# Adding the interpolated biases to the logits on TensorE and ScalarE in the first image's layer 0

## The chip, the cores and the metric

The kernel is one program on one core of a Trainium2 chip. The metric is the device time in microseconds (us) of one execution; lower is better. Each engine of the core (TensorE, written PE in the profile; VectorE, DVE; ScalarE, ACT; GpSimd, POOL; SyncE, SP) works through a queue of its own in the order in which the queue was laid out, and engines wait for one another through semaphores.

## The reference, cut to what matters

The network has four layers over four images of 32 x 32 positions and 384 channels. The change touches only layer 0, an attention whose keys are sampled at learned positions. Cut to the lines that matter:

```python
q = jnp.einsum('bhwc,cd->bhwd', x, w_q) + b_q
...
k = (xs @ w_k + b_k).reshape(Bq, n, HEADS, HC)
v = (xs @ w_v + b_v).reshape(Bq, n, HEADS, HC)
attn = jnp.einsum('bmhc,bnhc->bhmn', qh, k) * scale
disp = (ref.reshape(1, n, 1, 2) - pos.reshape(Bq * G, 1, n, 2)) * 0.5
bias = _bilinear_sample(rpe_img, disp)
attn = jax.nn.softmax(attn + bias, axis=-1)
out = jnp.einsum('bhmn,bnhc->bmhc', attn, v)
```

There are 6 heads of 64 channels and n = 1024 positions. For each image and head, `attn` is 1024 x 1024, and so is `bias`: each entry is a bilinear interpolation in a table, with weights that depend on the key alone.

## The kernel before, in words

**Two lanes.** `Front` computes layer 0 of an image, `Trunk` layers 1 to 3. Both are generators of instructions. `Net.layer0` writes out the whole front of image 0 before anything else; from then on the trunk of image b is written out interleaved with the fronts of the later images. So layer 0 of the first image stands alone, and that of the other three shares the engines with the trunk of the image before.

**Order on the engines.** The framework, Tile, lays out each engine's queue when the kernel is built: earlier code goes first where it can, and later code is moved up into what the framework takes for a gap. The trace shows that the order isn't the one in the code. `keep_in_program_order` pins single instructions; none in `head0` is pinned. A tag of a tile pool is a fixed number of slots: `bank` has 4 PSUM slots of 128 x 512, `lg` 13 SBUF slots, `z` 3, `win` 4, `tb` 2.

**The pass.** `Front.layer0` calls `head0(h, q)` for 6 heads and 2 halves of the queries: 12 passes an image. Everything is transposed: keys lie on the 128 partitions, queries on the free axis. A pass has 8 key tiles j (128 keys each) and 512 queries.

- *Bias of one key tile* (L733 to L752): POOL gathers a window of the table for each key (`win`, L734); ACT multiplies by one weight into `z` (L746), DVE adds the other row (L747); ACT multiplies by the column weight into `lg` (L751), DVE adds the other column (L752). Now `lg` holds the interpolated bias, 128 x 512.
- *Logits* (L754 to L761): PE multiplies the keys with the queries into a `bank` (L755); DVE adds the bank to `lg`, in place (L756); DVE keeps a running maximum over the key tiles in `rmax` (L759, L761).
- *Maximum over keys* (L765 to L780): PE transposes `rmax` in four pieces into a bank (L768), DVE reduces it (L772), POOL spreads the result on diagonals (L774), PE multiplies those with ones to have the maximum of each query on all partitions (L776), ACT copies it to `tb` (L780).
- *Softmax and values* (L784 to L798): for each of the 8 tiles DVE subtracts `tb` (L787), ACT takes the exponential (L788), PE multiplies with the values and with ones into one bank, `po`, in its two halves of 64 partitions (L790). Then ACT copies the output over the queries in `qpad` (L794) and the sums out (L797), and a DMA on SP's queue stores the sums (L798).
- After every second head `over_sums` (L801 to L822) loads the sums, has DVE invert them (L808), stores them, loads them spread over partitions and has DVE multiply the outputs (L821).

A float32 matmul stands in the trace as two records of MATMUL and two of LDWEIGHTS. A slot of `lg` is free again when L790 has read its tile, so 5 tiles of the next pass can have their bias ready while the 8 of this pass are in use. After the 12 passes `l0c` projects the output (`dense_t`, L376), adds it to the input (L432) and stores it; the trunk of image 0 begins from that.

Of the kernel before, what the change touches and what calls it, by code (L numbers as in the profile page):

```python
# [21 lines left out]
ALU = mybir.AluOpType  # L22
# [4 lines left out]
P = 128  # L27
# [37 lines left out]
def bc(ap, axis, n):  # L65

    u = ap.unsqueeze(axis)
    shape = list(u.shape)
    shape[axis] = n
    return u.broadcast_to(shape)  # L70


class Net:
# [183 lines left out]
    def layer0(self, b):  # L257

        if b == 0:
            for _ in self.front.layer0(b):  # L260
                pass
            self.done = self.ahead = 0.0
            self.fronts = (w for i in range(1, NB) for w in self.front.layer0(i))
# [135 lines left out]
class Front(Lane):  # L399


    def layer0(self, b):
        nc, v = self.nc, self.nc.vector
        with self.scope("l0"):
            self.qpad = self.wt([P, KC, PW, PW], "qpad")
            nc.gpsimd.memset(self.qpad, 0.0)

            self.kz = [self.wt([P, N], f"kz{r}") for r in range(2)]
            for r in range(2):
                nc.gpsimd.memset(self.kz[r][GC * (1 - r) : GC * (2 - r), :], 0.0)  # L410
            self.va = self.wt([P, NJ, C], "va")
            self.f = self.wt([P, 2, 2, NJ * G], "bias_f")
            self.widx = self.wt([P, 2, NJ * G], "widx", 1, I32)
            with self.scope("l0a"):
                yield from self.inputs0(b)
            with self.scope("l0b"):
                self.load_keys(0)
                for h in range(G):
                    if h + 1 < G:
                        self.load_keys(h + 1)  # L420
                    for q in range(2):
                        yield from self.head0(h, q)
                    if h % 2:
                        yield from self.over_sums(h // 2)
            with self.scope("l0c"):
                w = self.weights("w_out")
                for ko in range(KC):
                    rows = slice(ko * P, (ko + 1) * P)
                    x = self.wt([P, N], "res", 2)
                    nc.sync.dma_start(x, self.x0[b % 2][rows, :])  # L430
                    ps = self.dense_t(w, self.qpad, ko)
                    v.scalar_tensor_tensor(x, ps, self.col(C_BOUT, ko), x, ALU.add, ALU.add)  # L432
                    nc.sync.dma_start(self.x1[b % 2][rows, :], x)
                    yield 6
# [281 lines left out]
        rows = slice((h % 2) * GC, (h % 2 + 1) * GC)  # L716
        self.nc.sync.dma_start(self.kz[h % 2][rows, :], self.k0[h * GC : (h + 1) * GC, :])

    def head0(self, h, q):

        nc, v = self.nc, self.nc.vector
        f, kz, va = self.f, self.kz[h % 2], self.va
        k, r0 = h // 2, (h % 2) * GC
        rows = slice(r0, r0 + GC)
        other = slice(GC - r0, 2 * GC - r0)
        HH, HN = HW // 2, N // 2
        both = self.qpad[:, k, 1 + HH * q : 1 + HH * (q + 1), 1 : 1 + HW]
        queries = both[rows]
        logits = []
        rmax = self.wt([P, HN], "rmax", 2)  # L730
        for j in range(NJ):
            c = j * G + h
            win = self.wt([P, (HH + 1) * WROW], "win", 4)  # L733
            nc.gpsimd.indirect_dma_start(  # L734
                out=win,
                out_offset=None,
                in_=self.strips[:, :],
                in_offset=bass.IndirectOffsetOnAxis(
                    ap=self.widx[:, q, c : c + 1], axis=0
                ),  # L740
            )
            wv = win.rearrange("p (r c) -> p r c", c=WROW)
            sc = lambda i, t: f[:, i, t, c : c + 1]

            z = self.wt([P, HH, HW + 1], "z", 3)
            nc.scalar.activation(z, wv[:, 0:HH, 0 : HW + 1], AF.Copy, scale=sc(1, 1))  # L746
            v.scalar_tensor_tensor(  # L747
                z, wv[:, 1 : HH + 1, 0 : HW + 1], sc(0, 1), z, ALU.mult, ALU.add
            )
            lg = self.wt([P, HH, HW], "lg", 13)  # L750
            nc.scalar.activation(lg, z[:, :, 0:HW], AF.Copy, scale=sc(1, 0))  # L751
            v.scalar_tensor_tensor(lg, z[:, :, 1 : HW + 1], sc(0, 0), lg, ALU.mult, ALU.add)  # L752
            lf = lg.rearrange("p y x -> p (y x)")
            ps = self.bank()  # L754
            nc.tensor.matmul(ps, kz[:, j * P : (j + 1) * P], both, start=True, stop=True)  # L755
            v.tensor_tensor(lf, ps, lf, ALU.add)  # L756
            logits.append(lf)
            if j == 1:
                v.tensor_tensor(rmax, logits[0], lf, ALU.max)  # L759
            elif j > 1:  # L760
                v.tensor_tensor(rmax, rmax, lf, ALU.max)  # L761
            yield 3


        NI = HN // P  # L765
        ps = self.bank()
        for i in range(NI):
            nc.tensor.transpose(  # L768
                ps[:, i * P : (i + 1) * P], rmax[:, i * P : (i + 1) * P], self.ident
            )  # L770
        top = self.wt([P, NI], "top", 2)
        v.tensor_reduce(top, ps.rearrange("p (i n) -> p i n", i=NI), AX.X, ALU.max)  # L772
        diag = self.wt([P, NI, P], "diag", 1)
        nc.gpsimd.tensor_tensor(diag, bc(self.ident, 1, NI), bc(top, 2, P), ALU.mult)  # L774
        ps = self.bank()
        nc.tensor.matmul(  # L776
            ps, self.ones, diag.rearrange("p i n -> p (i n)"), start=True, stop=True
        )
        tb = self.wt([P, HN], "tb", 2)
        nc.scalar.copy(tb, ps)  # L780
        yield 3


        po = self.bank()  # L784
        for j in range(NJ):
            lf = logits[j]
            v.tensor_tensor(lf, lf, tb, ALU.subtract)  # L787
            nc.scalar.activation(lf, lf, AF.Exp)  # L788
            for out, w in ((rows, va[:, j, h * GC : (h + 1) * GC]), (other, self.ones[:, 0:GC])):
                nc.tensor.matmul(po[out, :], w, lf, start=j == 0, stop=j == NJ - 1)  # L790
            if j % 2:
                yield 2

        nc.scalar.copy(queries, po[rows, :].rearrange("p (y x) -> p y x", y=HH))  # L794
        o0 = other.start
        den = logits[0][o0 : o0 + 1, :]
        nc.scalar.copy(den, po[o0 : o0 + 1, :])  # L797
        nc.sync.dma_start(self.den[h][:, q * HN : (q + 1) * HN], den)  # L798
        yield 3
# [753 lines left out]
```

## Time and profile before

| what | value |
|---|---|
| median of three runs | 5029.74 us (5029.07 to 5034.31) |
| the profiled execution: device time / span | 5029.6 us / 5027.8 us |
| PE, DVE, ACT, POOL busy in the span | 86%, 63%, 48%, 19% |
| the passes of the first image, 225 to 605 us | PE 234.5, DVE 312.6, ACT 197.3, POOL 127.0 us busy of 380 |
| L756 in the whole kernel | 384 of 684 ns |
| L755 in the whole kernel | 768 records of 623 ns |
| L780 in the first image | 12 of 586 ns |

The start of the 12 copies into `tb` (L780) marks the passes of the first image: 255.9, 286.8, 315.5, 343.1, 388.2, 417.6, 446.0, 475.2, 520.5, 549.3, 578.4 and 605.0 us. They are read in the timeline of ACT. Eleven periods follow the first pass: nine from 26.6 to 30.8 us, with a mean of 28.7 us, and two of 45.1 and 45.3 us, which follow the `over_sums` of heads 0, 1 and 2, 3.

How to read it: a line of the page's groups names the line of code, the engine, the operation, output and input, and the count; then the busy time and the mean of one in ns; then how long the engine stood idle just before, and whom it waited for. In a timeline, a line gives the start, the duration, the engine and the instruction, with "x8" for eight merged; in brackets stands the idle time before it. PEclk is the share of TensorE's full clock that was granted.

### The profile page before, as it was taken

Reading aid. Unit: us, or ns where it says so; the run is one execution under the profiler, and the core shown is the slowest. Engines: PE = TensorE matmul, PEld = TensorE weight load, DVE = VectorE, ACT = ScalarE, POOL = GpSimd, SP = SyncE. Lnnn points to the kernel's source line nnn. Section 1 sums busy time; section 2 is a strip of 40 time slices with the busy share of each in tenths; the row PEclk is TensorE's granted clock in tenths of the full one; section 3 lists DMA queues with packets and bytes.
Section 4 is the critical chain, followed back from the end, with each engine's and each line's share of the span. In section 5 each row is a group of like instructions: output and inputs, shape, how many; then the busy total and the mean of one; then the engine's idle time right before and its main releaser. Section 6 shows DMA issues by size and latency. Waiting matters only on the chain. (4 is left out here: it accounts for less than half of the span.)

```text
span 5027.8 us, 47291 instructions
## 1 busy us (share of the span) xinstructions
PE 4315.1 (86%) x15788; PEld 1843.8 (37%) x15788; DVE 3178.1 (63%) x5743; ACT 2404.6 (48%) x4346; POOL 944.7 (19%) x946
## 2 busy tenths in 40 slices
PE   4466587899999988899999989789999998899998
PEld 2222242333333353333333444233333335234444
DVE  3477727577778725567777752657776872555544
ACT  2155424466666213466665412446666621566630
POOL 1523202211212002321122110321121200000000
PEclk7677787899999988799999989689999998799998
DMA  6322252311212143222121124231121214101001
GB/s 116 108 77 84 66 163 66 105 53 50 70 50 72 38 136 108 79 87 60 50 70 56 50 80 144 68 102 50 50 71 50 72 36 134 58 19 29 23 29 38
DMA packets 226707, 360.57 MB, mean 72 GB/s; under 512 B 116323, under 2 KB 163520, under 8 KB 226464
## 3 DMA queue, kind: packets, MB, share of 16 engines
q1 hardware_dynamic: 165448, 191.06, 12.6%
q0 software_dynamic: 39936, 145.53, 10.0%
q10 hardware_dynamic: 21080, 20.96, 1.8%
q8 instruction: 125, 2.05, 0.2%
q14 instruction: 118, 0.97, 0.1%
HBM read 279.55 MB, written 78.21 MB: 71 GB/s over the span
## 5 line engine op out<-in xcount | busy, mean ns | idle before, releaser
L1206 DVE SCALAR_TENSOR_TENSOR e<-bank,gam,e 128x512 f32<-128x512 f32 x768 | 562.8, 748 | 552.2 <-ACT gn L1205 247.4
L1197 PE MATMUL bank<-sim,sg 128*128 128x512 f32 (+3 forms) x2304 | 853.7, 507 | 5.1 <-DVE e L1206 5.1
L1044 ACT ACTIVATE big<-big,nmax 128x512 f32<-128x512 f32 x768 | 508.7, 662 | 420.7 <-DVE nmax L1039 383.8
L734 POOL DMA_INDIRECT win<-strips,widx x384 | 424.7, 1106 | 978.5 <-DVE z L747 409.4
L1175 ACT ACTIVATE e<-big 128x1024 f32<-128x1024 f32 x384 | 378.4, 1021 | 365.2 <-PE big L1167 355.5
L1031 PE MATMUL big<-k,q 32*128 32x512 f32 x1536 | 410.6, 748 | 148.8 <-ACT big L1044 81.2
L1197 PEld LDWEIGHTS bank<-sim,sg 128*128 128x128 f32 x2304 | 405.6, 198 | 360.2 <-issue 282.0
L1039 DVE TENSOR_REDUCE nmax<-big 128x2 f32<-128x1024 f32 x384 | 459.8, 1219 | 122.9 <-PE big L1031 85.4
L1167 PE MATMUL big<-qa,ka 64*128 64x512 f32 x1536 | 416.3, 626 | 15.9 <-ACT big L1044 9.7
L790 PE MATMUL bank<-lg,va 128*64 128x512 f32 x768 | 377.5, 639 | 38.4 <-ACT lg L788 38.3
L1152 POOL TENSOR_SCALAR sg<-sim,gam 128x512 f32<-128x512 f32 x192 | 152.9, 799 | 1309.5 <-PE bank L1197 957.6
L755 PE MATMUL bank<-qpad,kz 128*128 128x512 f32 x768 | 379.8, 623 | 19.6 <-DVE e L1206 10.3
L746 ACT ACTIVATE z<-win,bias_f 128x528 f32<-128x528 f32 x384 | 278.2, 738 | 207.2 <-DVE lg L752 120.6
L790 PE MATMUL bank<-lg,ones 128*64 128x512 f32 x768 | 376.8, 639 | 0.0
L752 DVE SCALAR_TENSOR_TENSOR lg<-z,bias_f,lg 128x512 f32<-128x512 f32 x384 | 292.9, 774 | 54.8 <-ACT lg L751 53.8
L747 DVE SCALAR_TENSOR_TENSOR z<-win,bias_f,z 128x528 f32<-128x528 f32 x384 | 294.3, 781 | 43.1 <-ACT z L746 25.7
L652 POOL DMA_INDIRECT gat<-pairs,sidx x192 | 208.3, 1085 | 580.5 <-DVE ix_fl L463 313.5
L756 DVE TENSOR_TENSOR lg<-bank,lg 128x512 f32<-128x512 f32 x384 | 257.2, 684 | 56.3 <-PE bank L755 53.8
L751 ACT ACTIVATE lg<-z,bias_f 128x512 f32<-128x512 f32 x384 | 270.7, 721 | 44.8 <-DVE z L747 33.5
L787 DVE TENSOR_TENSOR lg<-lg,tb 128x512 f32<-128x512 f32 x384 | 249.0, 704 | 68.0 <-ACT tb L780 67.9
L788 ACT ACTIVATE lg<-lg 128x512 f32<-128x512 f32 x384 | 222.0, 628 | 62.3 <-DVE lg L787 61.8
L1031 PEld LDWEIGHTS big<-k,q 32*128 32x128 f32 x1536 | 115.6, 209 | 343.0 <-ACT big L1044 170.8
(256 smaller groups left out, 5930.6 us busy)
## 6 DMA issues: line engine op xcount, KB each, us to landing
pairs<-xn SPq DMA_DIRECT2D x64, 192.0 KB
w<-in_gmat SPq DMA_DIRECT2D x16, 576.0 KB
w<-in_w_off SPq DMA_DIRECT2D x12, 576.0 KB
w<-in_Wqkv SPq DMA_DIRECT2D x12, 576.0 KB
a<-in_x SPq DMA_DIRECT2D x16, 384.0 KB
x<-a ACTq DMA_DIRECT2D x4, 1536.0 KB
k<-a SPq DMA_DIRECT2D x12, 512.0 KB
kz<-k SPq DMA_DIRECT2D x24, 256.0 KB
```

What stands on the lines that cost most here:

```text
L734: nc.gpsimd.indirect_dma_start(out=win, out_offset=None, in_=self.strips[:, :], in_offset=bass.IndirectOffsetOnAxis(ap=self.widx[:, q, c : ...
L747: v.scalar_tensor_tensor(z, wv[:, 1 : HH + 1, 0 : HW + 1], sc(0, 1), z, ALU.mult, ALU.add)
L752: v.scalar_tensor_tensor(lg, z[:, :, 1 : HW + 1], sc(0, 0), lg, ALU.mult, ALU.add)
L755: nc.tensor.matmul(ps, kz[:, j * P : (j + 1) * P], both, start=True, stop=True)
L790: nc.tensor.matmul(po[out, :], w, lf, start=j == 0, stop=j == NJ - 1)
L1031: nc.tensor.matmul(ps[c // 2][:, c % 2, :], self.q4[rows, i * P : (i + 1) * P], self.k4[rows, h * 512 : (h + 1) * 512], start=True, stop=True,
L1039: v.tensor_reduce(nmax[:, 2 * g : 2 * g + 2, i, h], ps[g], AX.X, ALU.max, negate=True)
L1044: nc.scalar.activation(ps[g][:, r, :], ps[g][:, r, :], AF.Exp, bias=nmax[:, c, i, h : h + 1], accum_out=den[:, c, i, h : h + 1],)
L1167: nc.tensor.matmul(ps[:, r, :], ka[rows, j * P : (j + 1) * P], qa[rows, cols], start=True, stop=True,)
L1175: nc.scalar.activation(e, ps, AF.Exp)
L1197: nc.tensor.matmul(ps[:, (mid - i0) * P :], sg[:, r, m, :], sim[:, r, m, mid * P : i1 * P], start=m == 0, stop=m == 1,)
L1206: v.scalar_tensor_tensor(e[:, r, :], ps, self.gam[:, 1:2], e[:, r, :], ALU.add, ALU.mult, accum_out=tot[:, r, h : h + 1],)
```

## The change

For the first image alone, `head0` gets a flag. With it, the matmul of keys and queries leaves its sum in the bank open; a second matmul, of the identity with the bias tile `lf`, adds the bias to it; and ScalarE copies the bank to `lf`. VectorE's addition is left out there. The running maximum reads `lf` as before. The other three images keep VectorE's addition.

```diff
-                        yield from self.head0(h, q)
+                        yield from self.head0(h, q, b == 0)
...
-    def head0(self, h, q):
+    def head0(self, h, q, alone):
...
-            nc.tensor.matmul(ps, kz[:, j * P : (j + 1) * P], both, start=True, stop=True)
-            v.tensor_tensor(lf, ps, lf, ALU.add)
+            nc.tensor.matmul(ps, kz[:, j * P : (j + 1) * P], both, start=True, stop=not alone)
+            if alone:
+                nc.tensor.matmul(ps, self.ident, lf, start=False, stop=True)
+                nc.scalar.copy(lf, ps)
+            else:
+                v.tensor_tensor(lf, ps, lf, ALU.add)
```

## The prediction

> **What bounds the kernel now.** I read the page first: over the span TensorE is busy 86% and VectorE 63%. Those are averages over stages, and the change touches one stage, so I then asked for the busy times between 225 and 605 us, where the passes of the first image lie, with the groups of that window, and last for the timeline of one pass.
>
> ```profile
> core 0: us, PE busy (x) PEld busy (x) DVE busy (x) ACT busy (x) POOL busy (x), PEclk, DMA share, GB/s
> 225.00:605.00 380.00, 234.53 (x616) 80.31 (x616) 312.60 (x478) 197.30 (x314) 127.02 (x105) 0.74 0.29 84
> ```
>
> ```profile
> L755 PE MATMUL bank<-qpad,kz 128*128 128x512 f32 x184 | 91.8, 647 | 8.8 <-DVE lg L756 8.8
> L756 DVE TENSOR_TENSOR lg<-bank,lg 128x512 f32<-128x512 f32 x96 | 64.9, 685 | 12.4 <-PE bank L755 12.2 <-issue 0.2
> L780 ACT COPY tb<-bank 128x512 f32<-128x512 f32 x11 | 6.4, 582 | 32.2 <-PE bank L776 32.2
> ```
>
> Here VectorE is busiest (82%), TensorE has 62%, ScalarE 52%. That looks like a stage that VectorE bounds and that shortens with 96 fewer instructions of VectorE. The timeline of one pass says more: who is late changes within the pass.
>
> ```profile
> 445.99 0.59 ACT L780 COPY tb<-bank 128x512 f32<-128x512 f32 x1 [0.18 <-PE bank L776]
> 446.60 4.91 DVE L787 TENSOR_TENSOR lg<-lg,tb 128x512 f32<-128x512 f32 x8
> ...
> 448.39 1.12 PE L790 MATMUL bank<-lg,va 128*64 128x512 f32 x1 [2.44 <-ACT lg L788]
> ...
> 458.40 7.16 PE L755 MATMUL bank<-qpad,kz 128*128 128x512 f32 x16
> ...
> 459.56 0.69 DVE L756 TENSOR_TENSOR lg<-bank,lg 128x512 f32<-128x512 f32 x1 [2.29 <-PE bank L755]
> ...
> 469.17 0.69 DVE L761 TENSOR_TENSOR rmax<-rmax,lg 128x512 f32<-128x512 f32 x1
> ...
> 469.91 1.11 PE L768 MATMUL bank<-ident,rmax 128*128 128x128 f32 x4 [4.36 <-DVE rmax L761]
> ...
> 475.17 0.59 ACT L780 COPY tb<-bank 128x512 f32<-128x512 f32 x1 [13.62 <-PE bank L776]
> ```
>
> From one copy into `tb` to the next, 29.2 us: (B) 2.4 us until the first L790; (C) TensorE without a break on L790, 448.39 to 458.40 = 10.0 us; 1.2 us to the first sum; (A) VectorE without a break, 8 sums and 8 maxima from 459.56 to 469.9 = 10.3 us; (B again) transposes, reduction, diagonal, ones, 5.3 us. VectorE decides A alone; TensorE decides C. VectorE's other work (bias, 16 instructions) lies under B and C, or before. At all eleven turns from pass to pass the L755 of the next pass come after the first L790 of this one: TensorE isn't used in B, though it stands idle there.
>
> **What the Trainium skill says.** "FP8 and Floating Point Precision", TensorE Precision Notes: true FP32 takes four passes through the array. "TensorE: Matmul & The Clock Gate", Part 1: back-to-back matmuls of 512 columns start 215.7 ns apart warm and 426.7 ns cold, so I estimate 0.86 and 1.71 us for one fp32 matmul. The trace agrees: in L755 above (7.16 - 0.59)/15 = 0.44 us a record, two records a matmul; while PEclk was 0.50 (449 to 454 us) L790's pairs started 0.85 us apart. The same part says that the clock falls back after an idle window of about 3.4 us and rises after as long a busy one; here it fell 2.3 to 5.2 us after the last matmul, and L790 ran cold for 6.0 us of its 10.0. "VectorE: DVE Perf Modes", the trn2 errata table, prices a ScalarE copy out of PSUM of 512 elements at 172 + 512 cycles of 1.2 GHz, 0.57 us; the trace has 0.58 for L780, which I use.
>
> **The change part by part.** Per pass:
>
> 1. *Removed:* 8 L756. They start 0.60 us from the next instruction, so 8 x 0.60 = 4.8 us of VectorE in A.
> 2. *Added on TensorE:* 8 identity matmuls, 2 records each at 0.43 us = 6.9 us; no pass of before has one. The lower end of its price is nothing (all of it in B's idle time), the upper 13.7 us (cold). I take 6.9: A then follows busy time on TensorE, so it is warm. The weights' loads (188 ns) are hidden in the 0.43.
> 3. *Added on ScalarE:* 8 copies, 0.58 us each, about 0.53 apart: 4.3 us. ScalarE stands idle 7 to 13 us around A, which hides them, except the last, which now lies between the last matmul and the last maximum. Were that cover gone it would be 4.3 us a pass.
> 4. *Added waits:* TensorE's identity matmul waits for L752; behind it are queued the next L755 and the transposes. ScalarE's copy waits for TensorE; behind it are queued L746, L751 and L788, for which VectorE and then TensorE wait. The maximum waits for the copy instead of the bank.
> 5. *PSUM, DMA, POOL:* the same number of banks and gathers. `po` holds one bank, so three turn: matmuls and copy hold one for 1.72 + 0.6 = 2.3 us, below 3 x 1.72. No cost.
>
> What is late next? In A VectorE has now 8 x 0.60 for maxima, but TensorE has 32 records, 32 x 0.43 = 13.8 us. So TensorE runs from the first L790 to the last identity matmul: 10.0 + 13.8 = 23.8 us. Then follow the copy, 0.64, the last maximum, 0.75, and B: transposes 0.85, reduction 0.80, diagonal 1.20, ones 1.56 (half-way between 2.08 cold and about 1.04 warm, as the idle time before it shrinks), and 2.4 to L790; 0.05 for waits. That is 8.25 us, and the pass takes 32.05 in place of 29.2: **+2.9 us**. Nine periods are of this kind: 9 x 2.9 = +26.
>
> *First pass:* VectorE-bound from 226 to 250 us with the bias inside; 4.8 us less work, against some 2.8 for the longer way to the last maximum and a cold start: -2.
>
> *The two periods with `over_sums`* (45.1 and 45.3 us): there VectorE's queue is stopped by L808 and L821.
>
> ```profile
> 490.51 0.25 DVE L808 RECIPROCAL dens<-dens 128x16 f32<-128x16 f32 x1 [9.82 <-DMA dens<-den]
> 496.03 0.69 DVE L821 TENSOR_TENSOR qpad<-qpad,lg 128x512 f32<-128x512 f32 x1 [4.02 <-DMA lg<-rden]
> ```
>
> After that VectorE works to 514 us before the transposes. Sums no longer queue behind L808, so TensorE and ScalarE go on with tiles whose bias is ready. At least 0, at most 9 us (the 4.8 and three biases that fit in earlier); I take 5: 2 x -5 = -10. The third stop comes after the last pass and stays.
>
> *ScalarE's order:* it waited 51.9 us for gathers in this window, 16 times, 32.1 of it once at the start; the others hold it 1.3 us each. Where such a wait stands ahead of a copy, TensorE has 2 x 1.72 us of slack in banks. Between 0 and 15 us; I take 4.
>
> Sum: +26 - 2 - 10 + 4 = **+18 us**. The execution's 5029.6 us becomes 5047.6, so 5048; the median, 5029.74, is the same to 0.2 us. I take the shift at its full size to the end: the trunk of image 0 begins from `l0c` after this stage, and the later images have the code of before. Their queues are laid out again, which I price at nothing, +-5.
>
> **The rivals.**
>
> *TensorE's new work moves into B (faster).* B leaves it 5.8 us idle a pass. If L755 and identity matmul of two tiles are laid there, A shortens by 2 x 1.72 = 3.4 us, and a TensorE that stays warm saves up to 3.1 us in C (10.0 to 6.9). From two tiles on, the sign turns: 2.9 - 3.4 = -0.5 a pass. With both, -3.6 x 9 = -32, and -8 of the other terms of the sum make -40; without warmth it is -4.5 - 8 = -12.5; half-way 5003. For it: banks and five biases are ready in B, ScalarE is idle. Against: at eleven of eleven turns L755 wasn't put there, with the same banks free. 0.20.
>
> *ScalarE's queue becomes the stop (slower still).* If a copy is laid ahead of exponentials, TensorE's L790 waits for ScalarE and ScalarE for TensorE, some 2.3 us (the time of one bank) in each of 12 passes: +28, 5076. For it: layout goes by estimates, and TensorE is cold in C. Against: ScalarE has 183 us to spare. 0.18.
>
> *The parts cancel:* `over_sums` yields 9 us each and ones and L790 run warmer by 1 us a pass: 18 - 8 - 9 = +1, 5031. 0.12.
>
> **How the numbers follow.** The forecast itself has 0.50, with its own range 5035 to 5060. The range, 5008 to 5080, reaches into the fast rival as far as leaves about 0.12 below and to the slow one's end with 0.08 above. What a measurement can tell from no change is 0.2%, 10 us: 5020 to 5040. Faster: 0.17 of the first rival. Same: 0.03 of it, the 0.12, and 0.10 of the forecast's lower edge. Slower: 0.40 and 0.18.
>
> **What would show it.** Right: in the changed profile A is one unbroken run of 32 records of TensorE from the last L790 on, VectorE idle between maxima, periods near 32 us; TensorE some 83 us busier (96 x 0.86) and VectorE 58 us less (96 x 0.60) in the stage; the two long periods near 40. Wrong: records of L755 before the first L790 of the pass ahead; periods under 28 us; L788 waiting behind copies; a difference after 650 us that the start of the trunk doesn't carry.

## The result and the profile after

The changed kernel takes 5053.21 us (median of five, 5048.15 to 5062.41); the kernel before, run beside it, 5029.74 us (5026.27 to 5035.15). The ratio is 1.0045, 95% interval 1.003 to 1.006: 23.5 us slower, where 18 were forecast. The profiled execution has a span of 5051.4 us, 23.6 more than before.

In the changed kernel the lines behind the edit stand five further on: L780 has become L785, L790 L795, L808 L813. The busy times between 225 and 605 us, the window shown above of before, in the same columns:

```profile
225.00:605.00 380.00, 295.13 (x774) 107.34 (x775) 249.18 (x374) 242.12 (x402) 118.32 (x103) 0.84 0.27 83
```

TensorE went from 234.5 to 295.1 us busy though the window now holds less than the whole stage, and VectorE from 312.6 to 249.2. The engine that was busiest was relieved, and the stage became longer. The groups of the added lines in that window (the columns: busy us and mean ns, then idle time ahead):

```profile
L758 PE MATMUL bank<-lg,ident 128*128 128x512 f32 x178 | 99.3, 646 | 20.0 <-DVE lg L753 14.9 <-issue 5.0
L756 PE MATMUL bank<-qpad,kz 128*128 128x512 f32 x170 | 91.1, 626 | 1.3 <-ACT lg L759 1.3
...
L759 ACT COPY lg<-bank 128x512 f32<-128x512 f32 x88 | 50.8, 578 | 38.3 <-PE bank L758 38.2
```

The identity matmul (L758) costs what the matmul of keys and queries (L756) costs, and ScalarE's copy waits for TensorE (38.2 us in all), hardly the reverse (1.3 us). The timeline of one pass, from its first L795 (the values, L790 before) to the next copy into `tb`:

```profile
289.94 1.11 PE L795 MATMUL bank<-lg,va 128*64 128x512 f32 x1 [2.06 <-ACT lg L793]
...
299.21 1.13 PE L756 MATMUL bank<-qpad,kz 128*128 128x512 f32 x2
...
312.20 1.02 PE L758 MATMUL bank<-lg,ident 128*128 128x512 f32 x2
...
313.26 0.58 ACT L759 COPY lg<-bank 128x512 f32<-128x512 f32 x1 [1.13 <-PE bank L758]
...
313.88 0.69 DVE L766 TENSOR_TENSOR rmax<-rmax,lg 128x512 f32<-128x512 f32 x1 [1.02 <-ACT lg L759]
...
314.62 0.66 PE L773 MATMUL bank<-ident,rmax 128*128 128x128 f32 x4 [1.40 <-DVE rmax L766]
...
317.25 1.13 PE L781 MATMUL bank<-diag,ones 128*128 128x512 f32 x2 [1.97 <-POOL diag L779]
318.41 0.58 ACT L785 COPY tb<-bank 128x512 f32<-128x512 f32 x1 [4.57 <-PE bank L781]
```

Read it against the pass shown before. From 289.94 to 313.22 us TensorE has no gap: 9.3 us of values, 14.0 us of 32 records for eight tiles. At the last maximum VectorE waits 1.02 us for ScalarE, whose copy has waited 1.13 us for TensorE: the queue behind everything is TensorE's. Then 5.2 us to the copy, and 2.0 to the next first L795.

The 12 copies into `tb` now start at 255.9, 287.9, 318.4, 349.0, 394.9, 425.4, 455.8, 486.1, 531.2, 561.7, 592.1 and 622.4 us. The nine normal periods have a mean of 30.6 us in place of 28.7, the two long ones are 45.9 and 45.1 in place of 45.1 and 45.3. The first addition behind the output projection of the first image (L432) starts at 650.58 us in place of 633.19: 17.4 us of the 23.6 arise in the stage. Behind it the queues hold the same instructions in the same order in both kernels, but for two places where TensorE has two matmuls exchanged; the remaining 6.2 us lie within the spread of the executions.

### The profile page after: what moved, and what is told of

The parts are those of the page before. It is cut to its first block, busy times and chain, and to the rows that moved or that the text cites. A ratio compares the mean times of both kernels' runs of the same rounds, so it can differ in the third digit from the quotient of the medians.

```text
span 5051.4 us, 47782 instructions
## 1 busy us (share of the span) xinstructions
PE 4405.0 (87%) x15980; PEld 1883.7 (37%) x15980; DVE 3118.8 (62%) x5647; ACT 2454.4 (49%) x4442; POOL 932.8 (18%) x946
## 3 DMA queue, kind: packets, MB, share of 16 engines
q8 instruction: 127, 2.08, 0.2%
## 5 line engine op out<-in xcount | busy, mean ns | idle before, releaser
L795 PE MATMUL bank<-lg,va 128*64 128x512 f32 x768 | 376.6, 638 | 38.1 <-ACT lg L793 38.1
L756 PE MATMUL bank<-qpad,kz 128*128 128x512 f32 x768 | 386.8, 618 | 13.5 <-DVE e L1211 11.7
L795 PE MATMUL bank<-lg,ones 128*64 128x512 f32 x768 | 375.9, 638 | 0.0
L753 DVE SCALAR_TENSOR_TENSOR lg<-z,bias_f,lg 128x512 f32<-128x512 f32 x384 | 290.0, 765 | 80.5 <-ACT lg L752 79.1
L792 DVE TENSOR_TENSOR lg<-lg,tb 128x512 f32<-128x512 f32 x384 | 249.2, 706 | 84.1 <-ACT tb L785 84.1
L752 ACT ACTIVATE lg<-z,bias_f 128x512 f32<-128x512 f32 x384 | 270.4, 722 | 38.7 <-DVE z L748 19.5
L1172 PEld LDWEIGHTS big<-qa,ka 64*128 64x128 f32 x1536 | 138.7, 189 | 270.7 <-issue 167.0
```

Source lines behind the costliest of these rows:

```text
L1172: nc.tensor.matmul(ps[:, r, :], ka[rows, j * P : (j + 1) * P], qa[rows, cols], start=True, stop=True,)
```

## The experiments

All are made from the changed kernel. They were measured in three groups, each with runs of the kernel before beside it, and its level differs between them (5004.98, 5017.23 and 5034.41 us), so a total is read as a ratio to the runs of before in its own group, also where the expectation gives absolute times. What a kernel does to the stage is read in its own trace, one execution each: "normal" is the mean of the nine normal periods, "long" the two others, "end" the start of the first L432.

| kernel | normal | long | end | ratio to before, 95% |
|---|---|---|---|---|
| before | 28.7 | 45.1, 45.3 | 633.2 | |
| changed | 30.6 | 45.9, 45.1 | 650.6 | 1.0045 (1.003 to 1.006) |
| changed again | 31.1 | 46.4, 46.4 | 657.8 | 1.0051 (1.0031 to 1.0071) |
| VectorE copies | 33.8 | 47.4, 47.2 | 689.2 | 1.0106 (1.008 to 1.0132) |
| bias not added | 26.5 | 42.1, 41.3 | 602.4 | 0.9934 (0.9918 to 0.9951) |
| identity twice | 37.7 | 48.4, 47.4 | 719.6 | 1.0176 (1.0159 to 1.0193) |
| two of eight tiles | 29.1 | 45.5, 44.9 | 635.6 | 1.0 (0.9988 to 1.0012) |
| before, own banks | 26.6 | 45.1, 45.2 | 610.8 | 0.9967 (0.9954 to 0.998) |
| changed, own banks | 22.8 | 44.2, 44.6 | 572.6 | 0.9871 (0.9854 to 0.9887) |
| the same again | 22.8 | 43.6, 43.9 | 573.7 | 0.9884 (0.9866 to 0.9902) |
| changed, others moved | 23.2 | 44.6, 45.1 | 582.6 | 0.9917 (0.9901 to 0.9934) |
| changed, po moved | 28.1 | 45.9, 46.2 | 630.6 | 1.0008 (0.9997 to 1.0019) |
| own banks, sums later | see text | none | | 0.9828 (0.981 to 0.9846) |

**Theory:** TensorE's added matmuls pace the pass, and the shared slots of `bank` keep them out of TensorE's idle time. **Rivals:** ScalarE's copy and its waits are the cost; or the work of TensorE has slack.

**Whose copy.**

```diff
-                nc.scalar.copy(lf, ps)
+                v.tensor_copy(lf, ps)
```

> The identity matmul stays, but VectorE copies the bank out instead of ScalarE (its 8 additions of before become 8 copies of the same length). Theory (TensorE's extra matmuls pace the pass): VectorE then has 8 x 0.60 for copies and 8 x 0.60 for maxima, 9.6 us, still below TensorE's 13.8, so the normal periods stay near 30.6 us and the total near the changed kernel's, 5048 to 5062 us. Rival (ScalarE's copy, its place in ScalarE's queue and its two hops make the pass longer): the 17 us come back, 5030 to 5040 us.

The ratio is 1.0106. The rival falls: taking ScalarE out of the chain gives nothing back, and the stage ends 39 us later. But the theory's own number was wrong too; the periods didn't stay at 30.6. Only the three just before a long period or the end are near 31 (30.9 to 31.2), the others 33 to 36 us. In those three VectorE's queue holds only copies and maxima beside TensorE's 32 records, and they are the fair comparison: ScalarE's hop costs nothing there. In the others biases lie between the copies, and everything that follows VectorE comes late. In one of them TensorE's 32 records end at 471.6 us, without a gap as elsewhere, and then:

```profile
474.27 0.66 PE L773 MATMUL bank<-ident,rmax 128*128 128x128 f32 x4 [2.66 <-DVE rmax L766]
...
478.19 0.95 POOL L735 DMA_INDIRECT win<-strips,widx  x1 [0.30 <-issue]
479.16 1.05 POOL L779 TENSOR_TENSOR diag<-ident,top 128x512 f32<-128x512 f32 x1
...
480.26 2.07 PE L781 MATMUL bank<-diag,ones 128*128 128x512 f32 x2 [5.34 <-POOL diag L779]
```

The transposes wait 2.66 us for the last maximum instead of 1.40, and the diagonal stands on POOL behind gathers, so that the ones wait 5.34 us instead of 1.97. The relief of VectorE is worth something even here, and ScalarE was the right engine for the copy.

**Without the added matmul.**

```diff
-            nc.tensor.matmul(ps, kz[:, j * P : (j + 1) * P], both, start=True, stop=not alone)
+            nc.tensor.matmul(ps, kz[:, j * P : (j + 1) * P], both, start=True, stop=True)
...
-                nc.tensor.matmul(ps, self.ident, lf, start=False, stop=True)
```

> The identity matmul is left out, so the biases are computed and not added to the logits; ScalarE still copies the bank and VectorE still has no addition. Theory: the run of TensorE after L790 falls from 32 records to 16, by 6.9 us, in the nine normal periods, which become about 24 us; the total falls by about 60 us, with a little from the other three passes, to 4975 to 4995 us. Rival (the copy is the cost): only a small fall, 5035 to 5050 us.

The stage ends 48.2 us earlier than that of the changed kernel; the theory's side, short of its 60, as only the same three periods fell to 24 us (23.5 to 23.8) and the others stayed at 27 to 30. In those three the identity matmuls cost 6.9 us a pass (30.4 to 23.6), their whole length; in the others the transposes wait 3.5 to 4.5 us for VectorE's last maximum instead of 1.4. This splits the change in two: moving the addition off VectorE, with ScalarE copying, gains 633.2 - 602.4 = 30.8 us; the identity matmuls cost 650.6 - 602.4 = 48.2 us. The difference is the 17.4.

**The added matmul twice.**

```diff
+                nc.tensor.matmul(ps, self.ident, lf, start=False, stop=False)
                 nc.tensor.matmul(ps, self.ident, lf, start=False, stop=True)
```

> The identity matmul runs twice, so the bias counts twice; nothing else is changed. Theory: 16 more records of 0.43 us in each pass, 6.9 us, at full size in the nine normal periods (about 37.5 us each) and between none and all in the other three: 62 to 83 us more than the changed kernel, 5115 to 5138 us. Rival (TensorE has slack and the copy or the queues decide): less than half of that, under 5090 us.

Normal periods of 37.7 us: 7.1 more than with one, where 16 records of 0.43 us are 6.9. The stage ends 69.0 us later and the ratio rises by 0.0131, some 66 us: both inside the forecast 62 to 83. The second matmul costs its whole length; the first cost 30.6 - 26.5 = 4.1 us in the mean of the nine, the rest of its 6.9 being covered by what VectorE would have needed anyway.

**The slots.** The logits of the first image go to the pool `big`, whose two slots are hardly used in this stage; the copy stays on ScalarE.

```diff
-            ps = self.bank()
+            ps = self.big()[:, 0:512] if alone else self.bank()
```

> The changed kernel, with the logits of the first image in the slots of the pool big, which stand empty in this stage, instead of in the pool bank that they share with the transposes, the diagonal and po. Theory (the pool's order keeps TensorE's work out of the idle time around the maximum): part of L756 and of the identity matmuls is laid between transposes and first L795, TensorE's 48 records of 0.43 us a pass then nearly fill it, and the normal periods fall from 30.6 to 24 to 27 us: 5000 to 5020 us. Rival (the order of the chain, not the pool, keeps it out, or the copies then stand in the way of the exponentials on ScalarE): periods of 30 us or more, 5045 us or more.

Normal periods of 22.8 us, under the forecast; the ratio is 0.9871. One pass shows why:

```profile
274.80 1.02 PE L781 MATMUL bank<-diag,ones 128*128 128x512 f32 x2
...
275.91 1.13 PE L758 MATMUL big<-lg,ident 128*128 128x512 f32 x2
...
276.59 0.57 ACT L785 COPY tb<-bank 128x512 f32<-128x512 f32 x1
...
276.88 1.02 PE L756 MATMUL big<-qpad,kz 128*128 128x512 f32 x2
...
277.74 1.02 PE L758 MATMUL big<-lg,ident 128*128 128x512 f32 x2
...
279.14 0.64 PE L795 MATMUL bank<-lg,va 128*64 128x512 f32 x1 [0.38 <-ACT lg L793]
```

L756 and L758 of the next pass stand between the ones (L781) and the first L795, where TensorE stood idle for 2.0 us; and that L795 takes 0.64 us in place of 1.11, as TensorE hadn't cooled: from 225 to 545 us the granted clock is 0.93, against 0.84 in the changed kernel's window. The L795 of this pass last 7.0 us instead of 9.3, so 2.3 us of what the pass gains are the clock's.

The same edit with VectorE's addition kept:

```diff
-            ps = self.bank()
+            ps = self.big()[:, 0:512] if alone else self.bank()
...
-            if alone:
-                nc.tensor.matmul(ps, self.ident, lf, start=False, stop=True)
-                nc.scalar.copy(lf, ps)
-            else:
-                v.tensor_tensor(lf, ps, lf, ALU.add)
+            v.tensor_tensor(lf, ps, lf, ALU.add)
```

(with `stop=True` on the first matmul)

> The kernel before (VectorE adds), with the logits of the first image in the slots of big. Theory: L755 then comes before the first L790 of the pass ahead, so the additions no longer wait for the end of L790, and VectorE's own work, about 25.8 us a pass, becomes the bound: normal periods of 25.5 to 27.5 us in place of 28.7, the total 12 to 30 us below before. The change would then be worth some 3 to 4 us a pass with its own banks, where it costs 1.9 with shared ones. Rival (VectorE's order isn't freed by the banks): periods stay at 28 to 29 us, the total within 10 us of before.

26.6 us, as the theory had it. So the change costs 1.9 us a pass with shared slots (28.7 to 30.6) and gains 3.8 with own ones (26.6 to 22.8).

**Which of the shared tiles.** Once the logits stay in `bank` and all three other tiles of the pass (transposes, diagonal, `po`) go to `big`; once `po` alone does.

```diff
+        bank = (lambda: self.big()[:, 0:512]) if alone else self.bank
...
-        ps = self.bank()
+        ps = bank()
...
-        ps = self.bank()
+        ps = bank()
...
-        po = self.bank()
+        po = bank()
```

> The changed kernel; the logits stay in bank with its 4 slots, and the transposes, the diagonal and po go to big. Theory (only the shared order of the pool matters, not how many slots the logits have): normal periods like those with own banks, 21.5 to 24 us, the total 60 to 70 us below before. Rival (the number of slots matters as well): with 4 slots in place of 2 the periods fall under 21.5 us, the total by 75 us or more.

```diff
-        po = self.bank()
+        po = self.big()[:, 0:512] if alone else self.bank()
```

> The changed kernel; only po goes to big. Theory (slots of a pool are given out in the order of the code, so L756 of the next pass can be laid as early as the last tile ahead of it in the same pool): L756 then stands between L781 and the first L795, in the idle 2 us there, but not earlier; one and a half tiles of 1.72 us leave the run after L795, and TensorE is warmer: normal periods of 27 to 29 us in place of 30.6, the total within 15 us of before. Rival (po's bank itself, held through L795, is what delays it): periods as with own banks, under 24 us.

With all three moved the normal periods are 23.2 us, as the theory had them: four slots do no more than two, it is the sharing that mattered. The total missed its forecast, though: it fell by 0.83%, some 42 us, not 60 to 70; the stage ends 10 us later than with own banks. With `po` alone 28.1 us, within the forecast: at six of the eleven turns TensorE's queue has two L756 and one L758 of the next pass between L781 and the first L795, at the others two or more of these matmuls, and at none anything earlier. That is what an order by slots predicts: a tile of `bank` isn't laid before the tile ahead of it in the code has its slot.

**Fewer tiles.**

```diff
-            if alone:
+            if alone and j in (2, 5):
                 nc.tensor.matmul(ps, self.ident, lf, start=False, stop=True)
                 nc.scalar.copy(lf, ps)
```

(with `stop` of the first matmul set to match)

> The changed kernel, with the identity matmul and ScalarE's copy for key tiles 2 and 5 alone; the other six are added on VectorE, and the banks are shared as before. Theory: the run after L795 is then 20 records on TensorE, 8.6 us, and 6 additions and 8 maxima on VectorE, 8.4 us, where before it was 10.3 us on VectorE behind a 1.2 us lead: normal periods of 26.5 to 28 us in place of 28.7, the total 5 to 25 us below before. Rival (any identity matmul costs its whole length, as the second one did): 2 x 0.86 a pass more than before, 15 us or more above it.

A miss: 29.1 us and a ratio of 1.0, neither the gain nor the loss. In one pass VectorE works without a real break from 432.4 to 443.3 us, 10.9 us where 8.4 were forecast: on 6 additions, 7 maxima (not 8, as the first key tile needs none) and four instructions of the bias, where the pass shown of before has one. So the time that two additions left was filled again, and the 0.43 us records ran beside it. A sum over one stretch of the pass was too simple where VectorE is the bound.

**The changed kernel again,** beside the runs with moved slots:

> The changed kernel as it is, so that it stands on the same chip as the others of this call. Theory: its stage of the first image ends 17 us later than before, 17 to 24 us in the total. Rival (the 6 us that the first measurement had beyond the stage are part of the change): 24 us or more in the total, with the stage again at 17.

The total is 29.6 us above before, but neither side had the stage: in this execution it ended 24.6 us after that of before, 7.2 us later than the first time, though the instructions are the same. The trace shows where most of it lies. The period after each long one took 32.4 us instead of 30.5: the clock rose later, so that L795 took 10.0 us instead of 8.6 and 8.7, and fell earlier, so that the ones took 2.08 us instead of 1.64 and 1.53. So the cost of the change in the stage is 17 to 25 us by two executions of it and one of before, and both ends (1.0034 and 1.0049) lie within both intervals. How much of the 23.5 us lies beyond the stage isn't settled.

**Own banks, and the sums later.**

```diff
                         yield from self.head0(h, q, b == 0)
-                    if h % 2:
+                        if b == 0 and q == 0 and h in (2, 4):
+                            yield from self.over_sums(h // 2 - 1)
+                    if h % 2 and (b > 0 or h == G - 1):
                         yield from self.over_sums(h // 2)
```

> The changed kernel with the logits in big, once more, beside the next one. 55 to 70 us below before, as measured.

> The same with own banks, and the first image's over_sums of heads 0, 1 and of heads 2, 3 written one pass later. Theory (in the two long periods VectorE's queue stands at L813 and L826 for a DMA's way out and back, with the biases of the next pass behind it): the two periods of 44 us fall to 24 to 30 us, the total by another 28 to 40 us, about 95 us below before. Rival (the long periods come from the next head's own data): they stay above 38 us, the total within 12 us of own banks alone.

The division of the sums now finds them nearly there, where it waited 10.16 us in the changed kernel:

```profile
340.09 0.25 DVE L815 RECIPROCAL dens<-dens 128x16 f32<-128x16 f32 x1 [0.82 <-DMA dens<-den]
```

No period above 32 us is left: the two that were long are 20.5 and 20.8 us, and the ones behind them, which now hold the sums, 30.8 and 31.8. The stage ends 25 us earlier than with own banks alone, a little less than the 28 to 40 forecast, and the total is 88 us below before: it is the fastest version here and beats both kernels.

## Why the prediction was right, and where its terms were not

The forecast was 5048 us, and the mechanism it gave is the one in the traces: once the additions have left VectorE, the 32 records of TensorE behind L790 end last, and they can't begin earlier because nothing of the next pass is laid before this pass's first L790. Why nothing is laid there the prediction left open; the slots of `bank` were the answer. Of its signs, TensorE was busy 74.9 us longer from 225 us to the end of the stage (83 forecast) and VectorE 57.9 us less (58 forecast). VectorE wasn't idle between the maxima, as it had expected: bias instructions moved in there.

- *The run of 32 records:* 13.8 us forecast, 14.0 measured.
- *C and B:* mis-sized. In the pass shown L795 took 9.3 us instead of 10.0, and from the last identity matmul to the next first L795 there were 7.2 us instead of 8.25. Of the latter, 0.4 us lie in the ones, which took 1.13 us, where 1.56 was taken, half-way between cold and warm; another 0.4 in the way from the copy into `tb` to L795, 2.0 us, where 2.4 was taken. That one isn't the change's: in before it is 2.0 us as well behind the copies at 286.8 and 475.2 us. The pass that the prediction was read from was a slow one, 29.2 us where the nine have a mean of 28.7. So the level was missed by 1.4 us (32.05 to 30.6), but a normal pass cost 1.9 us instead of 2.9: nine of them 17, not 26.
- *How warm TensorE was:* "TensorE: Matmul & The Clock Gate", Part 1, which the prediction used for the idle window of about 3.4 us, fits the trace in part. The gap ahead of the transposes shrank from 4.36 to 1.40 us, and they took 0.66 us instead of 1.11. But the clock fell all the same at 318.4 us, behind the ones, with no gap over 1.97 us ahead; and in the nine normal periods the ones took from 1.13 to 1.64 us, in two of the repeated run 2.08, with 1.9 to 2.0 us of idle time just ahead in every one.
- *The count of maxima:* a pass has 7, not 8; from 459.56 us VectorE has 8 sums, 7 maxima and one instruction of the bias. Nothing in the sum hung on it.
- *The two long periods:* this step failed. Forecast was -10, measured +0.6 together (+2.4 in the repeated run). The prediction had TensorE and ScalarE going on while VectorE stood at the sums' DMA, though its own list of added waits has the identity matmul behind L752. The trace of the changed kernel has:

```profile
360.49 3.71 PE L756 MATMUL bank<-qpad,kz 128*128 128x512 f32 x8
...
364.71 0.25 DVE L813 RECIPROCAL dens<-dens 128x16 f32<-128x16 f32 x1 [10.16 <-DMA dens<-den]
364.88 1.32 DVE L753 SCALAR_TENSOR_TENSOR lg<-z,bias_f,lg 128x512 f32<-128x512 f32 x2
...
365.59 1.98 PE L758 MATMUL bank<-lg,ident 128*128 128x512 f32 x4 [1.39 <-DVE lg L753]
...
371.48 2.07 PE L758 MATMUL bank<-lg,ident 128*128 128x512 f32 x2 [3.91 <-DVE lg L753]
```

  Four L756 fill the four slots, and the identity matmul behind them waits for a bias (L753) that stands in VectorE's queue behind L813, the later ones behind L826: the dependency on VectorE had only moved from the sum to the bias. And TensorE cooled meanwhile; the identity matmul at 371.48 us took 2.07 us for two records. Moving the sums' code later took the long periods away, so the sums that VectorE's queue meets there are their cause. That the sums' own two tiles also take slots of `lg`, away from the next biases, was not tested apart.
- *The first pass:* -2 forecast, 0 measured (255.9 us in both).
- *ScalarE's order:* 4 us forecast, none seen: the normal periods are 30.3 to 30.6 us but for the first, 32.0, which holds the load of a table (1.28 us), as in before.

So the stage's 17.4 us against the forecast's 18 is luck: the nine periods came out 9 us and ScalarE's order 4 us below the forecast, the two long periods 10.6 us and the first pass 2 us above it. The total was closer than the working deserved. Of the rivals, the fast one was right about its mechanism: with two tiles and more moved into B, the sign turns. It only needed slots of its own.

## What to carry to other kernels

Before work is moved off the busiest engine, follow one period of the trace from release to release and ask which engine ends each stretch: here the relief of an engine that was 82% busy was outweighed by work put where another had no gap. Idle time of an engine is worth something only if its queue can be laid into it; tiles that share a pool's slots can forbid that, and giving the moved work slots of its own turned a loss of 0.45% into a gain of 1.2 to 1.3%, of which the slots alone, with VectorE still adding, gave 0.33%. A wait that is taken off one engine often comes back through the next operand, as the bias behind the sums did.

## What the runs showed of the hardware

A copy of 128 x 512 float32 out of PSUM took 0.58 us on ScalarE and 0.69 us on VectorE.

The gap just ahead of a matmul didn't decide its clock. The matmul with the ones took 1.13 us after 1.97 us of idle time in the pass shown of the changed kernel. In the pass of before it took twice that after the same time:

```profile
473.05 2.08 PE L776 MATMUL bank<-diag,ones 128*128 128x512 f32 x2 [2.03 <-POOL diag L774]
```

Nor did the work ahead of it alone. In the repeated run of the changed kernel, behind the same 32 records without a gap and the same two gaps, it was slow as well:

```profile
423.46 0.66 PE L773 MATMUL bank<-ident,rmax 128*128 128x128 f32 x4 [1.40 <-DVE rmax L766]
426.09 2.08 PE L781 MATMUL bank<-diag,ones 128*128 128x512 f32 x2 [1.97 <-POOL diag L779]
```

The moments at which the clock changed tell more. In the first run PEclk fell to 0.50 at 287.7, 318.4 and 349.1 us and rose to 1.00 at 294.5, 325.2 and 356.0: steps of 6.8 and 23.9 us, which are 2 and 7 times 3.41. It rose at 400.3, 3.2 us after the first L795 of that pass, and fell at 424.2, during the ones; in the repeated run it rose at 404.1, 6.1 us after the first L795, and fell at 424.6, before the ones. So whether a matmul behind a gap ran fast hung also on where in these steps it came, and two executions of one kernel differed by it. What sets the steps is not shown.
